# A recurrent cell in four PSUM tiles instead of one, with its seeds copied by halves of the batch

## The chip, the cores and the metric

The kernel runs on one core of a Trainium2 chip. The metric is the time of one execution on the device, in microseconds (us); the median of three runs is quoted. The core has five engines with their own instruction streams, which wait for one another by semaphores: TensorE (PE; its weight loads are listed as PEld), VectorE (DVE), ScalarE (ACT), GpSimd (POOL) and SyncE (SP, which here only issues DMAs). Matmuls write to PSUM, a memory of eight banks of 512 float32 a partition; ACT and DVE read and write it too.

## The reference

A GRU over 128 time steps with a batch of 64 and 512 features, everything in float32; every fourth step (but not the last) the state is passed through a projection before it goes into the next step. The result is added to the input.

```python
def step(h, inp):
    x_t, prop = inp
    comb = concatenate([x_t, h])
    z = sigmoid(comb @ Wz + bz)
    r = sigmoid(comb @ Wr + br)
    h_cand = tanh(concatenate([x_t, r * h]) @ Wh + bh)
    h_new = (1.0 - z) * h + z * h_cand
    h_next = where(prop, tanh(h_new @ Wp + bp), h_new)   # prop: (t + 1) % 4 == 0 and t < 127
    return h_next, h_new
out = x + transpose(ys)                                  # ys: the h_new of all steps
```

## The kernel before

Each weight matrix of 1024 rows is split: the upper 512 rows (`wx`) meet the input x, the lower 512 (`wh`) meet the state. The x part does not depend on the recurrence. It is computed ahead, for groups of four steps and three gates at once, by two nested levels of a fast matrix product with seven multiplications in place of eight: GpSimd forms the sums of inputs (`sum_raw12`, `sum_s12`, `sum_s34` and so on) and recombines the products (`outer_...`) into `cp`, with bias; PE multiplies into four PSUM banks `scratch_q`, `scratch_r`, `scratch_a`, `scratch_x`; ACT (line 466) and DVE (lines 475 to 482) read those out. `G[t]` is the part of `cp` that belongs to step t.

The recurrent part of a step goes into PSUM. The batch of 64 is cut into two halves of 32 (`S = 2`), and the 512 features into four column groups of 128 (`NQ = 4`) which lie on the four quarters of the 128 partitions: one half of one gate is a block of 128 partitions x 128 columns. `gate(i, lT, w)` runs one gate: for each half, four slices of the contraction and four column groups, so 16 matmuls a half. In the profile each of these float32 matmuls counts as two, so a gate is 64 matmuls and 64 weight loads.

Before PE runs a gate, ACT has copied the x part of that step into the place in PSUM on which the matmuls accumulate: `seed(i, t)` (line 364). For the projection the bias takes that part (line 680). Where a gate lies within `rec`, one tile over four banks, is said by `pair(i)`: r in banks 0 and 2 (one bank a half), first 128 columns; the projection in the same two banks, next 128 columns; the candidate in banks 1 and 2, third 128 columns; z with both halves in bank 3.

The order of all engines' work is written out by hand (`manual_schedule`); each engine runs its instructions in the order of the program, and the framework adds the waits, from what each instruction reads and writes of each tile. A step of the loop over t does, in this order:

1. r: `gate(R, ...)`, then `read_out()` of scratch banks that are complete; for each half a sigmoid in place (line 658), r times h on DVE (659), a transpose to `rhT` on DVE (227); then `seed(R, t + 1)` for the next step.
2. z: `gate(Z, ...)`, sigmoid to SBUF (670) and 1 - z in place (671), `keep` = (1 - z) h on DVE (672), `seed(Z, t + 1)`, and before a projection the bias into its place (680).
3. `fill(places[0])`: so many units of the x part from `queue`, each 16 matmuls and 16 weight loads in the profile's count.
4. candidate: `gate(H_, rhT, ...)`, `read_out()`; for each half tanh in place (703), times z (704), plus keep to `h_new` (713), transpose to `hT` (227); then `seed(H_, t + 1)`, and `fill(places[1])`.
5. in projection steps: `gate(P_, ...)`, tanh (729) and transpose for each half.
6. GpSimd's sums for the x part, and the addition of h_new to the input (780), from where SP stores it.

How many units go into the two fills repeats every eight steps (98 units in all), with exceptions at the head and tail:

```python
PLACES = (
    (8, 3, 0), (3, 8, 0), (6, 8, 0), (6, 8, 0), (6, 4, 0), (4, 6, 0), (8, 6, 0), (8, 6, 0),
)
```

In the last six steps the first fill is empty and the second has five units at most; there the x part of the last two steps is computed plainly, from weights that are loaded again (`reload`).

Of the kernel before, what the change touches and what calls it, by code (L numbers as in the profile page):

```python
# [9 lines left out]
F32 = mybir.dt.float32  # L10
BF16 = mybir.dt.bfloat16
U16 = mybir.dt.uint16
AF = mybir.ActivationFunctionType
# [4 lines left out]
def kernel(  # L18
# [14 lines left out]
    nc = tc.nc  # L33
    B, T, D = x.shape
    H = h0.shape[1]
    P = 128
    S = 2
    V = B // S
    NQ = P // V
    J = H // NQ  # L40
    C = 2
# [5 lines left out]
    R, Z, H_ = range(3)  # L47
# [11 lines left out]
    two = ctx.enter_context(tc.tile_pool(name="two", bufs=2))  # L59
    ps_c = ctx.enter_context(tc.tile_pool(name="ps_c", bufs=1, space=PSUM))  # L60
# [19 lines left out]
    def part(q):  # L80
        return slice(q * V, (q + 1) * V)
# [16 lines left out]
    xr = {}  # L98
# [5 lines left out]
    bias_in = const.tile([P, 4, J], F32, name="bias")  # L104
# [11 lines left out]
    for h in range(S):  # L116
        nc.gpsimd.dma_start(
            out=h_init[:, h, :],
            in_=h0[ts(h, V), :].rearrange("b (q j) -> q b j", q=NQ),
# [22 lines left out]
    for q in range(NQ):  # L142
        nc.sync.dma_start(
            out=bias_in[part(q), 3, :],
            in_=bp[ts(q, J)].rearrange("(o n) -> o n", o=1).broadcast_to([V, J]),
# [1 line left out]

    rec = ps_c.tile([P, 4, 4 * J], F32, name="rec")  # L150

    def pair(i):
        if i == Z:
            return rec[:, 3, : S * J].rearrange("p (h n) -> p h n", h=S)
        if i == H_:
            return rec[:, 1:3, 2 * J : 3 * J]
        first = 0 if i == R else J
        return rec.rearrange("p (h two) n -> p h two n", two=2)[:, :, 0, first : first + J]

    P_ = 3  # L160
    scratch = [ps_c.tile([P, 4 * J], F32, name=f"scratch_{n}") for n in "qrax"]
    q_ps, r_ps, a_ps, x_ps = (
        s[:, : 3 * J].rearrange("p (m h v) -> p m h v", m=2, h=S) for s in scratch
    )

    bias = bias_in.rearrange("p i (c n) -> p c i n", c=C)

    def halves(ps):
        return ps.rearrange("p h (c n) -> p h c n", c=C)

    def spread(bank, rows, which):
        bank = bank.rearrange("p (i n) -> p i n", i=4)
        n = len(which)
        for q in range(NQ):
            nc.tensor.matmul(
                bank[part(q), 0:n, :],
                lhsT=ones,
                rhs=bias_row[:, rows, ts(q, J)],
                start=True,
                stop=True,  # L180
            )
        for j, i in enumerate(which):
            nc.scalar.copy(bias_in[:, i, :], bank[:, j, :])
# [4 lines left out]
    def idle(n):  # L188
        for i in range(n):
            nc.tensor.matmul(  # L190
                rec[part(i % NQ), i // NQ % 4, :],
                lhsT=zeros[:, :V],
                rhs=zeros,
                start=True,
                stop=True,
            )

    def products(ps, lhs, rhs, start=False):
        for q in range(NQ):
            nc.tensor.matmul(  # L200
                ps[part(q)],
                lhsT=lhs,
                rhs=rhs(q),
                start=start,
                stop=True,
                skip_group_check=True,
            )

    def gate(i, lT, w):
        for h in range(S):  # L210
            for k in range(K):
                products(
                    pair(i)[:, h, :], lT[:, h, ts(k, V)], lambda q: w[:, k, ts(q, J)]
                )

    def product(ps, lT, w, k, start=False):
# [9 lines left out]
    def turn(dst, src):  # L226
        nc.vector.transpose(out=dst, in_=src)  # L227

    def new_T(tag, name):
        return two.tile([P, S, P], F32, tag=tag, name=name)  # L230
# [123 lines left out]
    G = {}  # L354
# [5 lines left out]
                G[2 * q + b] = cp[q][:, :, b]  # L360

    def seed(i, t):
        if t < T:
            nc.scalar.copy(halves(pair(i)), G[t][:, :, :, i, :].rearrange("p c h n -> p h c n"))  # L364

    queue = []
    pending = []
# [1 line left out]
    def fill(n):  # L369
        for _ in range(min(n, len(queue))):  # L370
            unit, end = queue.pop(0)
            unit()
            if end is not None:
                pending.append(end)

    def read_out():
        while pending:
            pending.pop(0)()
# [185 lines left out]
    }  # L564

    idle(64)
    join_x(0, 0)
    idle(16)
    join_x(0, 1)
    idle(32)  # L570
    h = h_init
    hT = new_T("hT", "hT_init")
    both = [plain(0), plain(1)]
    for e in range(3):
        parts = [us[4 * e : 4 * e + 4] for us in both]

        queue.extend(sum(map(list, zip(*parts)), []) if e == R else sum(parts, []))
        fill(4)
        if e == H_:
            read_out()  # L580
            for i in range(3):
                seed(i, 0)
        fill(4)
        if e == R:
            spread(scratch[3], slice(0, 2), (R, H_))
            spread(scratch[1], slice(2, 3), (Z,))
            nc.gpsimd.tensor_sub(bias_d, bias[:, 1, 0:3, :], bias0)
        if e == Z:
            for half in range(S):
                turn(hT[:, half, :], h[:, half, :])  # L590
    read_out()
    for i in (1, 2, 3):
        sum_inner(i, nc.gpsimd)
# [1 line left out]
    for t in range(T):  # L595
        g, j = divmod(t, Q4)
# [23 lines left out]
        def join(n):  # L620
            if t == 0:
                join_x(0, 2 + n)
            elif t == 1:
                join_x(1, 2 + n)
            elif t == 2:
                join_x(2, n)
            elif t == 4:
                join_x(3, 2 * n)
                join_x(3, 2 * n + 1)
            elif duo >= 0 and u in (5, 6):  # L630
                join_x(even + 2, 2 * (u - 5) + n)
            elif duo >= 1 and u in (1, 3):
                join_x(odd, u - 1 + n)

        gate(R, hT, wh[R])
        if t == 1:
            for i in (5, 7):
# [15 lines left out]
            outer_u2(odd - 2)  # L653
        rh = two.tile([P, S, J], F32, tag="rh", name=f"rh_{t}")
        rhT = new_T("rhT", f"rhT_{t}")
        for half in range(S):
            r = pair(R)[:, half, :]
            nc.scalar.activation(r, r, AF.Sigmoid)  # L658
            nc.vector.tensor_mul(rh[:, half, :], r, h[:, half, :])  # L659
            turn(rhT[:, half, :], rh[:, half, :])  # L660
        if t != 3:
            seed(R, t + 1)
        if last:
            seed(H_, t)
        join(0)

        gate(Z, hT, wh[Z])
        z = two.tile([P, S, J], F32, tag="z", name=f"z_{t}")
        keep = two.tile([P, S, J], F32, tag="keep", name=f"keep_{t}")
        nc.scalar.activation(z, pair(Z), AF.Sigmoid)  # L670
        nc.scalar.activation(pair(Z), pair(Z), AF.Sigmoid, scale=-1.0)  # L671
        nc.vector.tensor_mul(keep, pair(Z), h)  # L672
        join(1)
        if t == 1:
            sum_raw34(1)
# [1 line left out]
            seed(R, t + 1)  # L677
        seed(Z, t + 1)
        if prop:
            nc.scalar.copy(  # L680
                pair(P_), bias_in[:, 3, :].unsqueeze(1).to_broadcast([P, S, J])
            )
        if last:
            nc.gpsimd.tensor_add(xr[g][:, j], xr[g][:, j], keep)
        if t == 0:
# [8 lines left out]
        if t == T - 7:  # L694
            reload()

        gate(H_, rhT, wh[H_])
        read_out()
        h_new = two.tile([P, S, J], F32, tag="h", name=f"h_{t}")
        hT = None if last else new_T("hT", f"hT_{t}")  # L700
        for half in range(S):
            c = pair(H_)[:, half, :]
            nc.scalar.activation(c, c, AF.Tanh)  # L703
            nc.vector.tensor_mul(c, c, z[:, half, :])  # L704
            if last:
                o = xr[g][:, j, half, :]
                nc.vector.tensor_add(o, c, o)
                (nc.sync, nc.scalar)[half].dma_start(
                    out=out[ts(half, V), t, :].rearrange("b (q n) -> q b n", q=NQ),
                    in_=o,  # L710
                )
                continue
            nc.vector.tensor_add(h_new[:, half, :], c, keep[:, half, :])  # L713
            turn(hT[:, half, :], h_new[:, half, :])
        if t < T - 2:
            seed(H_, t + 1)
        h = h_new
# [5 lines left out]
        if prop:  # L723
            gate(P_, hT, wp)
            read_out()
            h = two.tile([P, S, J], F32, tag="hprop", name=f"hprop_{t}")
            hT = new_T("hT", f"hpT_{t}")
            for half in range(S):
                nc.scalar.activation(h[:, half, :], pair(P_)[:, half, :], AF.Tanh)
                turn(hT[:, half, :], h[:, half, :])  # L730
            fill(places[2])
        if t == 0:
            join_x(1, 0)
# [48 lines left out]
        n = 0  # L782
        if t >= T - CHUNK:
            n = 3 if t == T - 2 else 0
        elif j == Q4 - 1:
            n = 4
        if n:
            for half in range(S):
                for q in range(NQ):
                    nc.sync.dma_start(  # L790
                        out=out[ts(half, V), t - n + 1 : t + 1, ts(q, J)],
                        in_=xr[g][part(q), j - n + 1 : j + 1, half, :],
                    )
        if j == 1 and g >= 1 and (g + 1) * Q4 < T:
            new_xr(g + 1)
# [47 lines left out]
```

## Time and profile before

| What | Value |
|---|---|
| Median of three runs | 1789.92 us (1787.52 to 1790.38) |
| Profiled execution: its time, its span | 1789.36 us, 1787.6 us |
| PE busy; its weight loads | 1378.8 us (77%), 51,920 matmuls; 1273.5 us (71%), 51,920 |
| DVE, ACT, POOL busy | 786.7 us (44%), 529.6 us (30%), 884.0 us (49%) |
| Mean granted clock of PE | 0.980 |
| Chain that ended last | PE 64%, DVE 14%, ACT 11%, issue 5%, rest 6% |
| Program of PE, fetched by DMA queue 8 | 406 packets, 6.65 MB |
| z activation (line 670) of steps 0, 8 and 120 | starts at 63.48, 189.82 and 1689.48 us |

The span is the time from the first to the last instruction of the profiled execution. A busy share is that of the whole span, and engines work side by side; a line like "L364" is a line of the kernel. "Idle before" is the time that an engine stood still ahead of an instruction, with the engine and line that ended the wait; "issue" means that the profile shows nothing that the engine waited for. Up to step 0's z the weights are still being loaded; from step 8 to step 120 the pattern of eight steps repeats fourteen times.

### The profile page before, as it was taken

Reading aid. Unit: us, or ns where it says so; the run is one execution under the profiler, and the core shown is the slowest. Engines: PE = TensorE matmul, PEld = TensorE weight load, DVE = VectorE, ACT = ScalarE, POOL = GpSimd, SP = SyncE. Lnnn points to the kernel's source line nnn. Section 1 sums busy time; section 2 is a strip of 40 time slices with the busy share of each in tenths; the row PEclk is TensorE's granted clock in tenths of the full one; section 3 lists DMA queues with packets and bytes.
Section 4 is the critical chain, followed back from the end, with each engine's and each line's share of the span. In section 5 each row is a group of like instructions: output and inputs, shape, how many; then the busy total and the mean of one; then the engine's idle time right before and its main releaser. Section 6 shows DMA issues by size and latency. Waiting matters only on the chain.

```text
span 1787.6 us, 111363 instructions
## 1 busy us (share of the span) xinstructions
PE 1378.8 (77%) x51920; PEld 1273.5 (71%) x51920; DVE 786.7 (44%) x2163; ACT 529.6 (30%) x1571; POOL 884.0 (49%) x1030
## 2 busy tenths in 40 slices
PE   6678777778777778777777777778787788777765
PEld 4577767777777777777777777777777777777755
DVE  0444444444444445444444444444444444444423
ACT  0123333233333333333333233333333323333221
POOL 2366555465454555545555554545545555454310
PEclk7799999999999999999999999999999999999999
DMA  2301111101111110111111111110111101111020
GB/s 103 110 24 39 39 28 40 38 17 38 39 39 28 38 31 26 39 29 50 28 29 34 32 39 28 39 39 16 40 28 50 28 24 32 40 27 28 16 79 14
DMA packets 114219, 66.36 MB, mean 37 GB/s; under 512 B 12604, under 2 KB 108988, under 8 KB 113756
## 3 DMA queue, kind: packets, MB, share of 16 engines
q1 hardware_dynamic: 113048, 58.90, 11.9%
q8 instruction: 406, 6.65, 1.5%
q14 instruction: 57, 0.47, 0.1%
q10 hardware_dynamic: 452, 0.20, 0.0%
q0 software_dynamic: 256, 0.14, 0.0%
HBM read 42.41 MB, written 16.78 MB: 33 GB/s over the span
## 4 chain that ended last, share of the span: by engine, by line
PE 64%; DVE 14%; ACT 11%; issue 5%; SPq 3%; DMA 2%; POOL 1%; ACTq 0%; DVEq 0%; POOLq 0%
PE rec L200 44%; PE scratch_x L200 5%; PE scratch_r L200 5%; PE scratch_q L200 5%; ACT rec L364 5%; DVE rh L659 4%; PE scratch_a L200 4%; SPq L93 2%; DVE rec L704 2%; DVE h L713 2%; DVE rhT L227 2%; ACT rec L658 2%; DVE keep L672 1%; DVE hT L227 1%; ACT rec L703 1%
## 5 line engine op out<-in xcount | busy, mean ns | idle before, releaser
L200 PE MATMUL rec<-wh,hT 128*32 128x128 f32 x12288 | 393.1, 278 | 200.3 <-ACT rec L364 187.9
L200 PEld LDWEIGHTS rec<-wh,hT 128*32 128x32 f32 x12288 | 337.3, 111 | 241.4 <-ACT rec L364 221.5
L200 PE MATMUL rec<-wh,rhT 128*32 128x128 f32 x8192 | 255.7, 274 | 33.0 <-ACT rec L364 22.6
L200 PEld LDWEIGHTS rec<-wh,rhT 128*32 128x32 f32 x8192 | 224.4, 110 | 46.7 <-ACT rec L364 29.7
L780 POOL TENSOR_TENSOR xr<-xr,h 128x256 f32<-128x256 f32 x127 | 92.4, 727 | 311.2 <-DVE h L713 286.9
L364 ACT COPY rec<-cp 128x256 f32<-128x256 f32 x384 | 144.6, 377 | 218.4 <-DVE h L713 87.1
L200 PE MATMUL rec<-wh,hpT 128*32 128x128 f32 x3968 | 121.5, 274 | 82.3 <-ACT rec L364 55.3
L200 PEld LDWEIGHTS rec<-wh,hpT 128*32 128x32 f32 x3968 | 105.4, 110 | 98.2 <-ACT rec L364 63.7
L510 POOL TENSOR_TENSOR cp<-mb,mb 128x768 f32<-128x768 f32 x75 | 136.6, 1821 | 65.4 <-DVE mb L482 61.8
L510 POOL TENSOR_TENSOR mb<-mb,mb 128x768 f32<-128x768 f32 x58 | 105.3, 1816 | 128.2 <-DVE mb L482 128.2
L672 DVE TENSOR_TENSOR keep<-rec,h 128x256 f32<-128x256 f32 x96 | 40.8, 425 | 278.7 <-ACT rec L671 278.7
L703 ACT ACTIVATE rec<-rec 128x128 f32<-128x128 f32 x256 | 67.1, 262 | 311.7 <-PE rec L200 217.3
L658 ACT ACTIVATE rec<-rec 128x128 f32<-128x128 f32 x256 | 67.1, 262 | 302.1 <-PE rec L200 256.4
L514 POOL TENSOR_TENSOR mb<-mb,bias 128x768 f32<-128x768 f32 x35 | 63.8, 1822 | 175.2 <-DVE mb L482 175.2
L670 ACT ACTIVATE z<-rec 128x256 f32<-128x256 f32 x128 | 49.1, 384 | 291.5 <-PE rec L200 291.5
L704 DVE TENSOR_TENSOR rec<-rec,z 128x128 f32<-128x128 f32 x256 | 76.7, 300 | 114.8 <-ACT rec L703 114.8
L466 ACT COPY cq<-scratch_q 128x384 f32<-128x384 f32 (+1 forms) x214 | 101.4, 474 | 22.5 <-PE scratch_q L200 22.1
L475 DVE TENSOR_TENSOR cx<-scratch_r,cx 128x384 f32<-128x384 f32 (+1 forms) x107 | 59.3, 554 | 98.1 <-ACT cx L466 98.1
L659 DVE TENSOR_TENSOR rh<-rec,h 128x128 f32<-128x128 f32 x192 | 56.0, 292 | 94.1 <-ACT rec L658 94.1
L510 POOL TENSOR_TENSOR cp<-cp,mb 128x768 f32<-128x768 f32 x29 | 53.0, 1829 | 87.7 <-DVE mb L482 86.6
L480 DVE TENSOR_TENSOR mb<-scratch_r,cq 128x384 f32<-128x384 f32 (+1 forms) x107 | 59.3, 554 | 79.9 <-ACT cq L466 62.0
L510 POOL TENSOR_TENSOR cp<-mb 128x768 f32<-128x768 f32 x47 | 85.9, 1827 | 12.3 <-ACT rec L364 10.9
(134 smaller groups left out, 2606.5 us busy)
## 6 DMA issues: line engine op xcount, KB each, us to landing
out_dram<-xr SPq DMA_DIRECT2D x249, 64.0 KB
xr<-in_x_dram SPq DMA_DIRECT2D x248, 64.0 KB
xs<-in_x_dram SPq DMA_DIRECT2D x240, 64.0 KB
wx<-in_L_cond_Wr_dram SPq DMA_DIRECT2D x7, 256.0 KB
wx<-in_L_cond_Wz_dram SPq DMA_DIRECT2D x7, 256.0 KB
wx<-in_L_cond_Wh_dram SPq DMA_DIRECT2D x7, 256.0 KB
wh<-in_L_cond_Wr_dram SPq DMA_DIRECT2D x4, 256.0 KB
wh<-in_L_cond_Wz_dram SPq DMA_DIRECT2D x4, 256.0 KB
```

The costliest lines, as they stand in the source:

```text
L200: nc.tensor.matmul(ps[part(q)], lhsT=lhs, rhs=rhs(q), start=start, stop=True, skip_group_check=True,)
L364: nc.scalar.copy(halves(pair(i)), G[t][:, :, :, i, :].rearrange("p c h n -> p h c n"))
L466: nc.scalar.copy(c[:, :nm], ps[:, :nm])
L475: nc.vector.tensor_add(T2[n][:, :nm], r_ps[:, :nm], T2[n][:, :nm])
L480: nc.vector.tensor_add(blocks(0, 1), runs(r_ps[:, :nm]), runs(q2[:, :nm]))
L510: nc.gpsimd.tensor_add(dst, a, b)
L514: nc.gpsimd.tensor_add(m, m, v.unsqueeze(1).to_broadcast([P, 4, 3, J // 2]))
L658: nc.scalar.activation(r, r, AF.Sigmoid)
L659: nc.vector.tensor_mul(rh[:, half, :], r, h[:, half, :])
L703: nc.scalar.activation(c, c, AF.Tanh)
L704: nc.vector.tensor_mul(c, c, z[:, half, :])
L780: nc.gpsimd.tensor_add(xr[g][:, j], xr[g][:, j], h_new)
```

## The change

The four banks of `rec` become four tiles, one bank each: `rec_r0` and `rec_r1` hold r (first columns) and the projection (next columns) of halves 0 and 1, `rec_h` the candidate of half 0, `rec_z` both halves of z. The candidate of half 1 lies in the third columns of `rec_r1`. So the layout in the banks is what it was. An instruction can now name one tile only, so the seeds of r, candidate and projection, which wrote both halves in one copy of 128x256, become two copies of 128x128, one a half; z's seed stays one copy. The order of the work is otherwise the same; the loop variable `half` is renamed `s_` in many places, which is left out here.

```diff
-    rec = ps_c.tile([P, 4, 4 * J], F32, name="rec")
-
-    def pair(i):
+    rec = [ps_c.tile([P, 4, J], F32, name=f"rec_{n}") for n in ("r0", "r1", "h", "z")]
+    zz = rec[3][:, :S]
+    P_ = 3
+
+    def half(i, h):
         if i == Z:
-            return rec[:, 3, : S * J].rearrange("p (h n) -> p h n", h=S)
+            return zz[:, h]
         if i == H_:
-            return rec[:, 1:3, 2 * J : 3 * J]
-        first = 0 if i == R else J
-        return rec.rearrange("p (h two) n -> p h two n", two=2)[:, :, 0, first : first + J]
-
-    P_ = 3
+            return (rec[2][:, 0], rec[1][:, 2])[h]
+        return rec[h][:, 0 if i == R else 1]
...
                 products(
-                    pair(i)[:, h, :], lT[:, h, ts(k, V)], lambda q: w[:, k, ts(q, J)]
+                    half(i, h), lT[:, h, ts(k, V)], lambda q: w[:, k, ts(q, J)]
                 )
...
     def seed(i, t):
-        if t < T:
-            nc.scalar.copy(halves(pair(i)), G[t][:, :, :, i, :].rearrange("p c h n -> p h c n"))
+        if t >= T:
+            return
+        src = G[t][:, :, :, i, :].rearrange("p c h n -> p h c n")
+        if i == Z:
+            nc.scalar.copy(zz.rearrange("p h (c n) -> p h c n", c=C), src)
+            return
+        for h in range(S):
+            nc.scalar.copy(half(i, h).rearrange("p (c n) -> p c n", c=C), src[:, h])
...
-        nc.scalar.activation(z, pair(Z), AF.Sigmoid)
-        nc.scalar.activation(pair(Z), pair(Z), AF.Sigmoid, scale=-1.0)
-        nc.vector.tensor_mul(keep, pair(Z), h)
+        nc.scalar.activation(z, zz, AF.Sigmoid)
+        nc.scalar.activation(zz, zz, AF.Sigmoid, scale=-1.0)
+        nc.vector.tensor_mul(keep, zz, h)
...
         if prop:
-            nc.scalar.copy(
-                pair(P_), bias_in[:, 3, :].unsqueeze(1).to_broadcast([P, S, J])
-            )
+            for s_ in range(S):
+                nc.scalar.copy(half(P_, s_), bias_in[:, 3, :])
```

More of the change, by code (lines that the diff above doesn't have):

```diff
@@ L166 @@
     bias = bias_in.rearrange("p i (c n) -> p c i n", c=C)
-    def halves(ps):
-        return ps.rearrange("p h (c n) -> p h c n", c=C)
     def spread(bank, rows, which):
@@ L190, in idle @@
             nc.tensor.matmul(
-                rec[part(i % NQ), i // NQ % 4, :],
+                rec[i // NQ % 4].rearrange("p c n -> p (c n)")[part(i % NQ)],
                 lhsT=zeros[:, :V],
@@ L588 @@
         if e == Z:
-            for half in range(S):
-                turn(hT[:, half, :], h[:, half, :])
+            for s_ in range(S):
+                turn(hT[:, s_, :], h[:, s_, :])
     read_out()
@@ L655 @@
         rhT = new_T("rhT", f"rhT_{t}")
-        for half in range(S):
-            r = pair(R)[:, half, :]
+        for s_ in range(S):
+            r = half(R, s_)
             nc.scalar.activation(r, r, AF.Sigmoid)
-            nc.vector.tensor_mul(rh[:, half, :], r, h[:, half, :])
-            turn(rhT[:, half, :], rh[:, half, :])
+            nc.vector.tensor_mul(rh[:, s_, :], r, h[:, s_, :])
+            turn(rhT[:, s_, :], rh[:, s_, :])
         if t != 3:
@@ L679 @@
         if prop:
-            nc.scalar.copy(
-                pair(P_), bias_in[:, 3, :].unsqueeze(1).to_broadcast([P, S, J])
-            )
+            for s_ in range(S):
+                nc.scalar.copy(half(P_, s_), bias_in[:, 3, :])
         if last:
@@ L700 @@
         hT = None if last else new_T("hT", f"hT_{t}")
-        for half in range(S):
-            c = pair(H_)[:, half, :]
+        for s_ in range(S):
+            c = half(H_, s_)
             nc.scalar.activation(c, c, AF.Tanh)
-            nc.vector.tensor_mul(c, c, z[:, half, :])
+            nc.vector.tensor_mul(c, c, z[:, s_, :])
             if last:
-                o = xr[g][:, j, half, :]
+                o = xr[g][:, j, s_, :]
                 nc.vector.tensor_add(o, c, o)
-                (nc.sync, nc.scalar)[half].dma_start(
-                    out=out[ts(half, V), t, :].rearrange("b (q n) -> q b n", q=NQ),
+                (nc.sync, nc.scalar)[s_].dma_start(
+                    out=out[ts(s_, V), t, :].rearrange("b (q n) -> q b n", q=NQ),
                     in_=o,
@@ L712 @@
                 continue
-            nc.vector.tensor_add(h_new[:, half, :], c, keep[:, half, :])
-            turn(hT[:, half, :], h_new[:, half, :])
+            nc.vector.tensor_add(h_new[:, s_, :], c, keep[:, s_, :])
+            turn(hT[:, s_, :], h_new[:, s_, :])
         if t < T - 2:
@@ L727 @@
             hT = new_T("hT", f"hpT_{t}")
-            for half in range(S):
-                nc.scalar.activation(h[:, half, :], pair(P_)[:, half, :], AF.Tanh)
-                turn(hT[:, half, :], h[:, half, :])
+            for s_ in range(S):
+                nc.scalar.activation(h[:, s_, :], half(P_, s_), AF.Tanh)
+                turn(hT[:, s_, :], h[:, s_, :])
             fill(places[2])
@@ L787 @@
         if n:
-            for half in range(S):
+            for s_ in range(S):
                 for q in range(NQ):
                     nc.sync.dma_start(
-                        out=out[ts(half, V), t - n + 1 : t + 1, ts(q, J)],
-                        in_=xr[g][part(q), j - n + 1 : j + 1, half, :],
+                        out=out[ts(s_, V), t - n + 1 : t + 1, ts(q, J)],
+                        in_=xr[g][part(q), j - n + 1 : j + 1, s_, :],
                     )
```

## The prediction

> **What bounds the kernel now.** I read the waits first, then one step in the timeline, then the instruction traffic. On PE the longest wait by far is for the copies that seed the recurrent banks (line, who is waited for, us in total, times, longest):
>
> ```profile
> PE rec L200 <- ACT rec L364: 302.2, 215, 2.1
> ACT rec L703 <- DVE h L713: 93.5, 127, 0.8
> ACT rec L658 <- DVE rh L659: 45.7, 128, 0.4
> ```
>
> The second and third lines say that the sigmoid or tanh of half 1 waits until VectorE is done with half 0, though the halves lie in different columns. One step in order of time (start, duration, engine, line, what, idle time before it):
>
> ```profile
> 900.20 1.96 PE L200 MATMUL rec<-wh,hT 128*32 128x128 f32 x64
> 902.28 0.26 ACT L658 ACTIVATE rec<-rec 128x128 f32<-128x128 f32 x1 [1.28 <-PE rec L200]
> 902.57 0.29 DVE L659 TENSOR_TENSOR rh<-rec,h 128x128 f32<-128x128 f32 x1 [0.97 <-ACT rec L658]
> 902.90 0.26 ACT L658 ACTIVATE rec<-rec 128x128 f32<-128x128 f32 x1 [0.36 <-DVE rh L659]
> 903.19 0.29 DVE L659 TENSOR_TENSOR rh<-rec,h 128x128 f32<-128x128 f32 x1
> 903.52 0.38 ACT L364 COPY rec<-cp 128x256 f32<-128x256 f32 x1 [0.36 <-DVE rh L659]
> 903.95 1.95 PE L200 MATMUL rec<-wh,hT 128*32 128x128 f32 x64 [1.79 <-ACT rec L364]
> ```
>
> The first sigmoid starts only after all 64 matmuls of r, although half 0 had ended after 32 of them. Then everything that touches `rec` runs in single file, and the z matmuls at 903.95, whose columns are in another bank and whose input hT was ready before r, wait for the seed of the next step's r. So `rec` is waited for as one thing. Tiles allocated apart are not: ACT copies out of scratch_q while PE writes scratch_r:
>
> ```profile
> 907.37 0.51 PE L200 MATMUL scratch_r<-wx,s 128*32 128x96 f32 x16
> 907.49 0.47 ACT L466 COPY cq<-scratch_q 128x384 f32<-128x384 f32 x1
> ```
>
> Next, eight steps (one period of `PLACES`), between two first sigmoids (us, then busy time and count of each engine):
>
> ```profile
> 878.44:984.48 106.04, 83.14 (x3232) 77.60 (x3232) 49.14 (x135) 33.45 (x99) 56.50 (x66) 1.00 0.14 36
> ```
>
> PE works 83 of 106 us; nobody else is above 57. What then stops PE from closing up is in the page's part 3 (packets, MB, share of 16 DMA engines):
>
> ```profile
> q8 instruction: 406, 6.65, 1.5%
> ```
>
> That is PE's program: 51,920 matmuls and as many weight loads in 406 packets, so 256 instructions a packet. The trace already shows PE halting ("issue") where it has run densely for a few us, and the halts are 128 matmuls (one packet) apart. Looking for a gap over 0.2 us exactly at a packet's first instruction I find about 90, and 24 times two in succession: the packet between took 3.41 to 4.02 us, 3.65 on average. These are some (stretch, length, PE busy and count):
>
> ```profile
> 962.36:965.83 3.47, 3.27 (x129) 1.00 0.02 5
> 1057.61:1061.35 3.74, 3.27 (x128) 1.00 0.34 93
> 1286.17:1289.64 3.47, 3.22 (x129) 1.00 0.02 5
> 1652.19:1655.96 3.77, 3.16 (x127) 1.00 0.02 4
> ```
>
> **The change, part by part.** *Waits.* With four tiles, z's bank no longer waits for the seed of r, and half 0 no longer for half 1. I lay a step out by the rows above, with W the first matmul of r, a gate 2.0 us (half 1.0), 0.08 from PE to ACT, 0.04 between other engines, ACT 0.26, DVE 0.30, transpose 0.31. r of half 0 ends W+1.0, its transpose is done at W+2.05; half 1 W+2.0 and W+3.05; the seeds of r follow rh, the last done at W+3.0. z runs W+2.0 to 4.0 with no wait (its seed is a step old). Then come the `places[0]` fill units (32 instructions, 0.33 us each: 0.66 for 64), so h half 0 starts at W+4.0 at the earliest, with its input 1.9 us old. The candidate's half 0 ends at Y-1.0 (Y the end of that gate), its tanh at -0.66, product, sum and transpose at Y+0.35; half 1 at Y+1.4. `places[1]` covers that: three units already give Y+1.0 for r's half 0 and Y+2.0 for half 1. Where three VectorE adds of a batch stand ahead (0.55 each) the chain ends up to 1.5 us later, at Y+2.9 at worst after a step with `places[0]` of 3, and there `places[1]` is 8 (2.6 us) and half 1 is wanted at Y+3.6. In a projection step P's half 0 activation and transpose (0.7 us) lie beside its half 1. So PE loses no wait in a full step.
>
> *The shared bank.* r1 holds r, P and the candidate of half 1, so the candidate's half 1 waits for the seeds there: of r W+3.0; of P, after z's two activations, keep and seed (X+1.75, X the end of z), X+2.3. It is wanted at X+1.0 plus the fill: in full steps with P the fill is 8 or 6 units, 2.0 us or more. Cost nothing; without that fill (one P step of the tail) 1.3.
>
> The Trainium skill, PSUM — Partial Sum Buffer ("PSUM bank collisions raise a hardware error"), says to guard by bank and not by address, which speaks against three gates in one bank; by it the price is the 1.3 us just named, and no run here shows a gate in a bank of its own.
>
> *Copies.* A seed of 128x256 takes 377 ns; two of 128x128 by the row of the same size (262) take 524, so 147 more, for r and candidate each step and P each fourth: 18 in eight steps, 2.6 us on ACT, which is then busy 36 of 93. ACT works ahead of PE by over 1 us where these stand; uncovered, they would cost their 0.15 each. No DMA, no POOL instruction and no matmul is added or moved. POOL's tightest delivery I find is s (done 918.47, read by PE at 923.88): 5.4 us, of which PE's gaps between (0.72, 1.85 and 0.42) go, so 2.4 stay.
>
> *What is late next.* Gates 26 x 2.0 and 98 units x 0.33 are 84.4 us for eight steps. The program of these steps is 6464 instructions, 25.3 packets; at 3.65 us that is 92.2. I expect PE to be paced by its instruction packets. A packet of fill runs 2.6 us and would wait, one of gates runs 4.0 and would not; most hold both, so I take the average (kept wholly apart, 13 x 4.0 + 12.3 x 3.65 would be 97). Some 4 more PE wait instructions a step add 0.13 packet, 0.5 us: 93 us per eight steps. Between the ends 3.41 (87 us) and 4.02 (102) I take the mean of the 24, since the regime is the same one made permanent.
>
> The Trainium skill, Runtime: NRT & Kernel Launch ("Instruction fetch mechanics"), calls the cost of crossing from one block of instructions to the next "mostly hidden". By it the eight steps would take 84.4 and the whole some 1440; the halts above differ, and I go by them.
>
> *Sum.* The profiled run took 1789.36 us, with a span of 1787.6 (the median of the three runs is 1789.92, 0.03% more). Between the z activations of step 8 (189.82) and step 120 (1689.48) lie 14 periods, 107.1 us each: 14 x (107.1 - 93) = 198 saved. Head (63.5 to 189.8): 30.6 packets at 3.65 are 112 of its 126, but loads hold it until 72 and POOL is on its chain from 110 to 136; between 0 and 14, I take 8. Tail (98.1 us): the last six steps have no first fill and up to five units; by the layout above a step takes 7.1 to 7.7 (10.4 with P) for 11.4 to 15.4 now, and ends when the chain of half 1 does. Step 120 and 121 at 11.5 and 10.7, then 7.4, 10.4, 7.1, 7.7, 7.1, 7.3: 69, plus an allowance of 2 for the reloaded weights: 27 saved. Together 233: 1556 us.
>
> **The rivals.** (A) The forecast: PE is paced by packets at 3.5 to 3.85 us: 89 to 98 per period, 1500 to 1630. (B) The packets come ahead after all; for it: three quarters of the boundaries show no gap; against: the gaps come just where PE has run densely, and elsewhere a wait for a seed gave the fetch its time. 85 us per period, 14 x 22.1 and 39 in head and tail, 349 saved: 1440. (C) Fetching slows as other transfers are squeezed into less time (of the rows shown, the one beside 93 GB/s took 3.74 and those at 5 GB/s 3.47, though one at 4 took 3.77): 3.95, near the longest pair, gives 100.3 per period, 14 x 6.8 and 35, 130 saved: 1659. (D) The other side, and the change not doing what it says: the four tiles are waited for as one. Then nothing is saved and each seed on the path is two copies, 0.15 us longer: before z 128 times, before r or P some 100 times: 34 us, 1823. Against it stands the scratch row above. It decides if z's matmuls still follow the seed of r; and A itself turns over at 4.2 us per packet, where 25.3 packets fill today's 106.
>
> **How the numbers follow.** A 0.77, B 0.07, C 0.11, D 0.05. The time is A's, 1556; A's ends hold most of its 0.77, and reaching half way to B and to C's 1659 brings the range to 1470 to 1660. About 0.2% (4 us) can be told from no change: faster 0.94, same 0.01 (C at its worst), slower 0.05.
>
> **What would show it.** Right: the line "PE rec <- ACT rec L364" falls from 302 us to under 20; z's matmuls follow r's directly; the first sigmoid starts about 1.1 us after r's first matmul; eight steps take 89 to 98 us with PE busy near 83; "issue" becomes PE's largest wait, at every packet; q8 still near 406 packets. Wrong: PE waiting for ACT or DVE once a step (D, or a wait on r1), POOL's sums arriving after PE asks, or eight steps under 87 (B).

## The result and the profile after

The changed kernel takes 1574.98 us (median of four runs, 1573.8 to 1575.51); the kernel before, beside it, 1788.77 (1787.52 to 1790.38). The ratio is 0.880, 95% interval 0.879 to 0.882: 12% faster. The profiled execution took 1573.8 us. In two later comparisons, on other chips, the same changed kernel took 0.892 and 0.900 of before; the first experiment shows where that time goes. Every ratio below is to runs of before in the same comparison.

From the page of the changed kernel: the span; busy time of each engine; PE's program (packets, MB, share of 16 DMA engines); the chain that ended last, by engine.

```profile
span 1572.0 us, 111797 instructions
...
PE 1369.3 (87%) x51920; PEld 1261.9 (80%) x51920; DVE 776.7 (49%) x2163; ACT 561.7 (36%) x1858; POOL 885.4 (56%) x1030
...
q8 instruction: 407, 6.67, 1.8%
...
PE 83%; issue 11%; SPq 3%; DMA 2%; POOL 1%; ACT 0%; DVE 0%; POOLq 0%; DVEq 0%; ACTq 0%
```

PE does the same work in nearly the same busy time as before (1378.8 us there); ACT and DVE, together 25% of the chain before, are gone from it, and "issue" has risen from 5% to 11%. PE's waits (us in total, times, longest):

```profile
PE rec_r L197 <- issue: 51.1, 92, 1.4
PE scratch_q L197 <- issue: 26.4, 42, 1.2
PE scratch_x L197 <- issue: 23.4, 42, 1.1
PE scratch_r L197 <- issue: 22.5, 47, 1.0
PE rec_h L197 <- issue: 18.5, 28, 1.5
PE rec_z L197 <- issue: 9.9, 24, 0.8
...
PE scratch_a L197 <- issue: 8.1, 20, 0.8
...
PE rec_r L197 <- ACT rec_r L684: 2.3, 2, 1.2
```

The 302 us of waiting for a seed of a gate are down to nothing. What is left are 160 us of "issue", in which PE is not seen to wait for any engine, spread over whatever PE happens to run. The last line is the one wait on a seed that remains: the candidate's half 1 waits twice (at 119 and at 1536 us) for the projection's seed, in the bank that r, projection and candidate share. Places in one step (start, duration, what, idle before):

```profile
844.81 1.96 PE L197 MATMUL rec_r<-wh,hT 128*32 128x128 f32 x64
...
845.93 0.26 ACT L661 ACTIVATE rec_r<-rec_r 128x128 f32<-128x128 f32 x1 [1.00 <-PE rec_r L197]
...
846.56 0.61 PE L197 MATMUL rec_z<-wh,hT 128*32 128x128 f32 x14
...
847.32 1.58 PE L197 MATMUL rec_z<-wh,hT 128*32 128x128 f32 x49
...
851.34 0.57 PE L197 MATMUL scratch_x<-tt,s 128*32 128x96 f32 x17 [0.84 <-issue]
855.13 0.60 PE L197 MATMUL scratch_x<-tt,o 128*32 128x96 f32 x18 [0.52 <-issue]
859.34 0.74 PE L197 MATMUL rec_r<-wh,hT 128*32 128x128 f32 x18 [1.04 <-issue]
```

The sigmoid of r's first half starts 1.12 us after r does, while PE is at the second half; z's matmuls begin at 846.56, as r ends, and not after a seed. The breaks at 847.32, 851.34, 855.13 and 859.34 are some 4 us apart, in a gate, in input products and in r: they follow the count of instructions, not the kind of work. Take every 256th instruction of PE (matmuls, weight loads and semaphore instructions in order of time), the first of each packet: at 360 of some 407 such boundaries it starts over 0.2 us after the instruction before it, 260 us in sum; before there were 94, with 63 us. Call a packet limited if it has such a gap at both ends. There are 327, and they take 3.74 us on average, from 3.3 to 4.35.

The transfers of queue 8 show what PE waits for. In a limited packet the transfer of the next one starts 1.25 us after the packet's first instruction and takes 1.10 us, and PE goes on 1.39 us after the transfer's end (means; the last lies between 1.23 and 1.56 in nine of ten). At the 310 boundaries of the kernel before that have no gap, the packet had been there longer: its transfer had ended 2.8 us ahead (median). So a limited packet lasts until its successor has come: 1.25 us until the successor's transfer starts, and 2.5 us from there.

Stretches from z of step 0 to z of step 8, from there to z of step 120, and to the end (us; busy time and count of PE, PEld, DVE, ACT, POOL; granted clock; DMA share; GB/s):

```profile
63.48:179.92 116.44, 101.23 (x3918) 94.98 (x3914) 61.01 (x158) 35.34 (x118) 75.53 (x87) 0.99 0.18 52
179.92:1501.99 1322.07, 1171.30 (x45201) 1086.61 (x45195) 679.37 (x1891) 498.20 (x1641) 783.87 (x910) 1.00 0.14 38
1501.99:1572.00 70.01, 60.05 (x2171) 56.56 (x2170) 30.69 (x98) 23.74 (x87) 13.05 (x12) 0.99 0.20 61
```

1322.07 / 14 = 94.43 us per eight steps, of which PE is busy 83.7 (1171.30 / 14).

### The profile page after: what moved, and what is told of

It reads as the page before. It is cut to its first block, busy times and chain, and to the rows that moved or that the text cites. A ratio compares the mean times of both kernels' runs of the same rounds, so it can differ in the third digit from the quotient of the medians.

```text
span 1572.0 us, 111797 instructions
## 1 busy us (share of the span) xinstructions
PE 1369.3 (87%) x51920; PEld 1261.9 (80%) x51920; DVE 776.7 (49%) x2163; ACT 561.7 (36%) x1858; POOL 885.4 (56%) x1030
## 3 DMA queue, kind: packets, MB, share of 16 engines
q1 hardware_dynamic: 113048, 58.90, 13.5%
## 4 chain that ended last, share of the span: by engine, by line
PE 83%; issue 11%; SPq 3%; DMA 2%; POOL 1%; ACT 0%; DVE 0%; POOLq 0%; DVEq 0%; ACTq 0%
PE rec_r L197 27%; PE rec_z L197 15%; PE scratch_x L197 10%; PE scratch_q L197 10%; PE scratch_r L197 10%; PE rec_h L197 7%; PE scratch_a L197 5%; SPq L93 3%; DMA wh<-in_L_cond_Wh_dram 1%; DMA wh<-in_L_cond_Wr_dram 1%; DMA xr<-in_x_dram 0%; POOL cp L513 0%; POOL mb L517 0%; DVE keep L675 0%; ACT z L673 0%
## 5 line engine op out<-in xcount | busy, mean ns | idle before, releaser
L197 PE MATMUL rec_r<-wh,hT 128*32 128x128 f32 x6144 | 206.7, 273 | 32.4 <-issue 31.8
L197 PE MATMUL rec_z<-wh,hT 128*32 128x128 f32 x6144 | 207.7, 273 | 11.5 <-issue 9.9
L197 PEld LDWEIGHTS rec_r<-wh,hT 128*32 128x32 f32 x6144 | 176.7, 110 | 44.3 <-issue 43.2
L197 PEld LDWEIGHTS rec_z<-wh,hT 128*32 128x32 f32 x6144 | 180.3, 110 | 22.7 <-issue 22.1
L197 PE MATMUL rec_h<-wh,rhT 128*32 128x128 f32 x4096 | 156.0, 273 | 21.8 <-issue 18.5
L197 PE MATMUL rec_r<-wh,rhT 128*32 128x128 f32 x4096 | 157.4, 273 | 15.7 <-issue 12.7
L661 ACT ACTIVATE rec_r<-rec_r 128x128 f32<-128x128 f32 x256 | 67.1, 262 | 248.9 <-PE rec_r L197 248.9
L197 PEld LDWEIGHTS rec_h<-wh,rhT 128*32 128x32 f32 x4096 | 123.5, 110 | 31.5 <-issue 26.3
L197 PEld LDWEIGHTS rec_r<-wh,rhT 128*32 128x32 f32 x4096 | 127.0, 110 | 24.0 <-issue 20.1
L367 ACT COPY rec_r<-cp 128x128 f32<-128x128 f32 x384 | 102.7, 268 | 103.7 <-DVE h L715 68.9
```

Of the source, the lines that this page charges most:

```text
L197: nc.tensor.matmul(ps[part(q)], lhsT=lhs, rhs=rhs(q), start=start, stop=True, skip_group_check=True,)
L367: nc.scalar.copy(half(i, h).rearrange("p (c n) -> p c n", c=C), src[:, h])
```

## The experiments

Theory: the four tiles took the waits for seeds away, and PE is now paced by its instruction packets; its own matmuls have time to spare. Rivals: PE's work itself is the bound; a chain of waits between gates still is; the gain is not from the tiles but could be had by order alone.

**The changed kernel again, on two other chips** (after_again, after_beside; no edit).

> The changed kernel as it is, on the chip of the experiments that follow. From the ratio 0.880 of its first comparison: 0.878 to 0.883 of before, some 1580 us where before takes 1794. Its use is the step: 14 periods of eight steps of 94.4 us each, about 360 of some 407 packet boundaries with a gap of over 0.2 us on TensorE.

> The changed kernel beside the next three runs. It took 0.880 of before where it was first compared and 0.900 in the comparison with rz_merged, where a limited packet took 3.83 us in place of 3.72; so 0.875 to 0.905 here, 1570 to 1625 us, and lower the shorter the packet is: 1 us of time per eight steps for each 0.04 us (25.3 packets).

Measured: 1614.01 us, ratio 0.900 (0.896 to 0.903); and 1605.47, ratio 0.892 (0.889 to 0.895). The first lies above what was expected of it (1580). The kernel before hardly differs between the comparisons (1789 to 1801). The table sets the mean time of a limited packet beside the time of eight steps; its parts are the start of the next packet's transfer, the transfer, and the time from its end to PE's next instruction.

| Comparison | Gaps at boundaries | Limited packets | us each | of these: start, transfer, to PE | x 25.3 | eight steps |
|---|---|---|---|---|---|---|
| first | 360 | 327 | 3.74 | 1.25, 1.10, 1.39 | 94.7 | 94.4 |
| after_beside | 372 | 346 | 3.82 | 1.31, 1.12, 1.39 | 96.7 | 96.2 |
| after_again | 376 | 357 | 3.87 | 1.33, 1.15, 1.39 | 98.0 | 97.5 |

The fourteen periods of after_again:

```profile
183.75:1549.14 1365.39, 1172.52 (x45201) 1086.13 (x45195) 679.92 (x1891) 498.34 (x1641) 785.36 (x912) 1.00 0.14 36
```

PE's work is the same (83.8 us for 83.7); what grew is the packet's time, in the start and the length of the transfer. The last two columns agree in good part because they must: most packets are limited. That the fetch sets the pace, and is not merely as long, is for the next two experiments to show. Why it is slower in one comparison than in another stays open. The expectations speak of packets of 3.72 and 3.83 us: the fourteen periods give 3.72 and 3.84 if gaps of over 1.2 us are left out. There is no ground for that, since at 23 of the first comparison's 24 such gaps PE is not seen to wait for any engine either.

The kernel before has a gap at a quarter of its boundaries only, and so hardly feels it.

**Thinner matmuls, same instructions** (thin_gates, repeated beside the changed kernel as thin_beside).

```diff
-                    half(i, h), lT[:, h, ts(k, V)], lambda q: w[:, k, ts(q, J)]
+                    half(i, h)[:, : J // 2], lT[:, h, ts(k, V)],
+                    lambda q: w[:, k, q * J : q * J + J // 2],
```

> The changed kernel with every recurrent gate and projection computed over 64 of its 128 columns a block (the other half of those products is left out). The number of PE instructions and all waits stay. Theory 1 (packets of instructions pace PE): the same time as the changed kernel, 1560 to 1580 us. Rival (PE is paced by the running of its matmuls): a gate of 2.0 us falls to 1.2 or less, 26 gates in eight steps, so some 20 us per eight steps and about 1290 us in all.

> As thin_gates (gates and projection over 64 of their 128 columns, the other half of these products left out; the same instructions), now beside the changed kernel on one chip. Packets pace TensorE: within 2% of the changed kernel, though TensorE's busy time is 340 us shorter. If the matmuls' own time counted, 150 us or more below it.

Measured: 1598.91 us, ratio 0.891 (0.888 to 0.894); and 1602.71, ratio 0.890 (0.886 to 0.894), against 0.892 (0.889 to 0.895) for the changed kernel beside it: no difference. (The first lies above its 1560 to 1580, which came from the first comparison's 1575.) From the page of the second run:

```profile
PE 1037.7 (65%) x51920; PEld 947.1 (59%) x51920; DVE 761.1 (47%) x2163; ACT 561.3 (35%) x1858; POOL 883.1 (55%) x1030
...
PE 59%; issue 32%; SPq 3%; DMA 2%; POOL 1%; DVE 1%; ACT 1%; ACTq 0%; POOLq 0%; DVEq 0%
```

A quarter of PE's busy time is gone, over 330 us, and "issue" has taken nearly all of it. A limited packet takes 3.81 us here and 3.82 in the changed kernel beside it, and eight steps 96.8 and 96.2, though PE is busy in only 62.7 of the 96.8. What a matmul does is not what paces PE; that it is an instruction is.

**More instructions, next to no work** (more_instr). The tile of zeros, whose buffer was used again, also gets one that stays.

```diff
+        for i in range(64):
+            nc.tensor.matmul(
+                rec[3][part(i % NQ), 3, 0:8], lhsT=zeros[:, :V], rhs=zeros[:, :8],
+                start=False, stop=True, skip_group_check=True,
+            )
         gate(Z, hT, wh[Z])
```

> The changed kernel with 64 tiny matmuls of zeros (8 columns) more a step, ahead of z, into columns that nothing reads: 128 instructions, half a packet, with hardly any data. Theory 1: half of 3.7 us a step in 128 steps, 225 to 240 us more, about 1810 us. Rival (the running of matmuls paces): 64 pairs at no more than the 20 ns that a pair of fill takes, so at most 165 us more and by their width far less, 1590 to 1740.

Measured: 1847.42 us, ratio 1.030 (1.027 to 1.033): the whole gain of the change is lost, more than the 1810 us expected. The program of PE, and the fourteen periods:

```profile
q8 instruction: 471, 7.72, 1.8%
```

```profile
198.79:1769.47 1570.68, 1252.75 (x52382) 1158.85 (x52376) 681.06 (x1891) 499.54 (x1640) 781.62 (x907) 1.00 0.12 32
```

Eight steps took 112.2 us, and PE was busy in 89.5 of them. 457 of some 471 boundaries show a gap, and a limited packet took 3.83 us. In thin_gates, on the same chip, it took 3.79 and eight steps 96.0: 25.3 + 4 packets of 3.79 us are 111.1 of the 112.2. So a packet costs about the same whether it holds the kernel's matmuls or, in part, these. The 1810 went by 3.7 us a packet and by the time of the first comparison.

**Fewer instructions, the same columns** (rz_merged). r and z multiply the same h, so their weights go into one tile and a matmul takes 128 columns of each.

```diff
-    wh = [const.tile([P, K, H], F32, name=f"wh_{i}") for i in range(3)]
+    whrz = const.tile([P, K, 2, H], F32, name="wh_rz")
+    wh = [whrz[:, :, 0], whrz[:, :, 1], const.tile([P, K, H], F32, name="wh_2")]
...
+    def gate_rz(lT):
+        for h in range(S):
+            for k in range(K):
+                products(
+                    rec[h][:, 0:2, :], lT[:, h, ts(k, V)], lambda q: whrz[:, k, :, ts(q, J)]
+                )
...
-        if i == Z:
-            return zz[:, h]
         if i == H_:
-            return (rec[2][:, 0], rec[1][:, 2])[h]
-        return rec[h][:, 0 if i == R else 1]
+            return rec[2 + h][:, 0]
+        return rec[h][:, {R: 0, Z: 1, P_: 2}[i]]
```

From step 1 on `gate_rz` stands in place of the two gates; z, 1 - z and `keep` are made by halves, and one copy of 128x256 seeds r and z of a half.

> r and z read the same h, so their weights go into one tile and one matmul computes 128 columns of each (256 columns, the same number of columns in all): 128 instructions a step fewer, four packets fewer in eight steps. The four PSUM tiles become two with r, z and projection of one half of the batch each, and two with a half of the candidate each; keep and the seeds are made by halves. Theory (packets pace TensorE): 25.3 - 4 = 21.3 packets of 3.72 us are 79 us per eight steps, less than the 84 us that the matmuls take now; TensorE's own work becomes the bound and a period takes 85 to 91 us in place of 94.4. 14 periods save 50 to 130 us; the tail, which has no other work to put behind r, loses up to 10. Together 1450 to 1535, most likely 1480. Rival 1 (the gaps are not the instructions' but the chain's from gate to gate): the period stays at 94 or grows, since r of the second half now ends 2 us later in a step: 1575 to 1620. Rival 2 (a matmul of 256 columns runs at a lower rate than two of 128): TensorE's busy time rises above 1400 us and the time stays above 1560.

Measured: 1396.11 us (1394.04 to 1398.72), ratio 0.778 (0.775 to 0.780), against 0.900 for the changed kernel beside it: a further 13.5%, and below all that was expected. Busy times and the program of PE; PE's longest waits; and the fourteen periods:

```profile
PE 1314.7 (94%) x43792; PEld 1159.4 (83%) x43792; DVE 794.3 (57%) x2291; ACT 568.0 (41%) x1988; POOL 887.8 (64%) x1030
...
q8 instruction: 343, 5.62, 1.7%
```

```profile
PE rec_rz L195 <- issue: 11.5, 24, 0.9
PE scratch_q L195 <- issue: 10.8, 20, 1.0
```

```profile
168.93:1327.35 1158.42, 1119.82 (x38040) 995.31 (x38036) 695.12 (x2004) 503.05 (x1752) 787.93 (x915) 1.00 0.16 42
```

64 packets fewer, 82.7 us per eight steps, and PE is busy in 80.0 of them (97%). Gaps at packets fell from 376 (311 us) in the changed kernel beside it to 122 (73 us), and at the other boundaries the packet's transfer had ended 1.9 us ahead (median). The theory said that PE's own work would be the bound, with 21.3 packets at 79 us well below it. But at this comparison's 3.87 us they are 82.4, as long as what was measured: PE's work and its packets are now so close that this run does not tell which of them bounds it. Where the expectation of 1480 was too high: eight steps took 82.7 for the 85 to 91 expected, 32 to 116 us in fourteen; the tail saved 3 us (69 for 72 beside it) where a loss of up to 10 was expected, and the head, of which nothing was said, 14 (106 for 120). PE's work was taken as unchanged, 84 us; it is 80.0. One part is seen in the rows, 62 wide matmuls in 3.62 us, 58 ns each, for two of 30.6 ns (64 in 1.96), about 1.4 us in eight steps; the rest was not told apart.

**z alone in a tile of its own** (z_own, repeated beside the changed kernel as z_own_beside): r, projection and candidate stay in one tile of three banks, seeded whole.

```diff
-    rec = ps_c.tile([P, 4, 4 * J], F32, name="rec")
+    rec = ps_c.tile([P, 3, 4 * J], F32, name="rec")
+    rec_z = ps_c.tile([P, 4 * J], F32, name="rec_z")
```

> One part alone: z in a tile of its own, r, projection and candidate in one tile of three banks, seeds in whole copies. Theory 1 (PE is then paced by its instruction packets, 25.4 per eight steps at 3.7 us): the gap before z goes (2.1 us a step), those left, before r, P and after P, are some 6 us per eight steps and lie mostly beside the fetching: 95 to 98 us per eight steps, about 1617 us in all, so three quarters of the gain. Rival (each wait removed pays for itself, the halves as much as z): half of the gain, about 1680 us.

> As z_own (z in a tile of its own, one three-bank tile for the rest, whole seeds), now beside the changed kernel on one chip: 1615 to 1645 us. What is asked is its share of the change's gain: 75% if the changed kernel takes 1575 here, 90% if it takes 1615. Theory (the packets pace both): the share is 80 to 95%, since what z_own keeps of waits lies under the packets for the most part. Rival (the other waits add to it in full): 70 to 78%.

Measured: 1633.83 us, ratio 0.911 (0.907 to 0.914), nearer to the theory's 1617 than to the rival's 1680; and 1630.93, ratio 0.905 (0.901 to 0.909), beside the changed kernel's 0.892 (0.889 to 0.895). So 0.095 of 0.108: this one separation brings 88% of the gain (82 to 95% from the ends of the intervals), inside the theory's 80 to 95 and outside the rival's 70 to 78. Its waits show why the rest brings little:

```profile
PE rec L201 <- issue: 50.0, 76, 1.4
PE rec L201 <- ACT rec L365: 36.4, 45, 1.5
PE scratch_q L201 <- issue: 28.1, 43, 1.4
PE scratch_r L201 <- issue: 27.2, 51, 1.1
PE rec L201 <- DVE hpT L228: 27.1, 30, 1.1
```

Some 64 us of waits for ACT and DVE remain, but the whole is only 25 us longer: gaps at packets are 222 us in sum, for 291 in the changed kernel beside it. A packet can arrive while PE waits.

**The same cover by order alone** (fill_first): the kernel before, with three units of input products moved ahead of z.

```diff
+        early = 3 if duo >= 0 and t < T - 10 else 0
+        fill(early)
         gate(Z, hT, wh[Z])
...
-        fill(places[0])
+        fill(places[0] - early)
```

> The kernel before, with its one PSUM tile and whole seeds, but in steps 3 to 117 three units of the input products (0.6 us each) are issued ahead of the z gate and three fewer behind it. If the wait that the change removed was only z waiting for the sigmoid of r, its reads and its seed (1.8 us a step), then 1.8 us of work put into it does the same without new tiles: a period falls from 107.1 us towards the packets' pace of 94 and the time to 1600 to 1660 (other waits of the one tile, as r's on the candidate's seed, stay). Rival: the products behind z covered the chain from r to the candidate, so the wait comes back there: the time stays within 2% of before (1760 to 1830).

Measured: 1731.11 us, ratio 0.964 (0.960 to 0.967). Both expectations missed it. The first line is PE's wait for the seeds, 302 us before; the others are one step:

```profile
PE rec L200 <- ACT rec L364: 233.0, 251, 2.0
```

```profile
1021.13 0.84 PE L200 MATMUL scratch_a<-wx,o 128*32 128x96 f32 x32
...
1021.44 0.26 ACT L658 ACTIVATE rec<-rec 128x128 f32<-128x128 f32 x1 [1.73 <-PE rec L200]
...
1021.79 0.51 PE L200 MATMUL scratch_r<-wx,s 128*32 128x96 f32 x16
...
1022.06 0.26 ACT L658 ACTIVATE rec<-rec 128x128 f32<-128x128 f32 x1 [0.36 <-DVE rh L659]
...
1022.74 0.38 ACT L364 COPY rec<-cp 128x256 f32<-128x256 f32 x1 [0.41 <-DVE rh L659]
...
1023.17 1.95 PE L200 MATMUL rec<-wh,hT 128*32 128x128 f32 x64 [0.86 <-ACT rec L364]
...
1026.83 1.69 PEld L200 LDWEIGHTS rec<-wh,rhT 128*32 128x32 f32 x64 [0.27 <-ACT rec L364]
```

Three units are 1.0 us, not 1.8 as the expectation took (0.6 for a unit, which takes 0.33), and halve the wait at z, from 1.8 to 0.86. The units are then missing behind z, where the candidate waits for z's seed in the same tile: more waits, 251 for 215. Work moved between two waits covers one or the other; separate tiles remove both. This is one order of many: that no order alone could do it is not shown.

**The split seeds alone** (copies_only), and the same with work in the wait ahead of z (copies_fill, which adds the edit of fill_first).

```diff
-            nc.scalar.copy(halves(pair(i)), G[t][:, :, :, i, :].rearrange("p c h n -> p h c n"))
+            src = G[t][:, :, :, i, :].rearrange("p c h n -> p h c n")
+            if i == Z:
+                nc.scalar.copy(halves(pair(i)), src)
+                return
+            for h in range(S):
+                nc.scalar.copy(pair(i)[:, h].rearrange("p (c n) -> p c n", c=C), src[:, h])
```

> One part alone: the seeds by halves, all four banks still one tile. If the tile decides, no wait goes and each seed on the path is 0.15 us longer, before z 128 times and before r or P some 100 times: about 1823 us. If the split of the copies were what helps, it would come down towards 1575; if seeds were off the path, 1789.

> copies_only (one PSUM tile, seeds by halves) with three units of the input products moved ahead of z, as in fill_first. copies_only lost 130 us against before where the copies' length gives 34, and its granted clock fell from 0.98 to 0.93. Theory (the clock is halved for want of work on TensorE in the wait ahead of z, and work in that wait keeps it): the clock is 0.975 or more and the time is that of fill_first plus the copies, 0.964 x 1793 + 34 = 1763 (1745 to 1790). Rival (the split copies cost 130 us in whatever order): about 1860, clock near 0.93.

Measured: copies_only 1924.77 us, ratio 1.072 (1.070 to 1.074), four times the loss that the copies' length gives; copies_fill 1791.61, ratio 0.995 (0.992 to 0.997). The mean granted clock (the share of TensorE's full clock) of copies_only was 0.930, with 66 stretches of mostly 3.4 us at half clock after the loading, 231 us together (before: 9, 31 us; the changed kernel: one, at its end). Two gates of it, in the second of which the clock has just fallen:

```profile
895.94 1.96 PE L200 MATMUL rec<-wh,hT 128*32 128x128 f32 x64 [0.74 <-ACT rec L369]
899.94 2.74 PE L200 MATMUL rec<-wh,hT 128*32 128x128 f32 x64 [2.04 <-DVE xT L240]
```

PE's busy time rose from 1378.8 to 1476.3 us, 97 more for the same matmuls, and the span by 131.0. PE's waits together (gaps over 0.15 us) rose by 34 us, 399 to 433, which is what the copies were priced at. The 97 fit the clock: 200 us more at half speed can lengthen PE's work by 100 at most. In copies_fill the clock is back at 0.978; against fill_first (run on another chip) PE is busy 20 us longer (1399.4 for 1379.5) and the span is 60 longer (1789.0 for 1728.5), so 40 are left for the copies and their order. The theory had the clock right and the time (1763) 29 us too low; the rival's 1860 is out. The Trainium skill, TensorE: Matmul & The Clock Gate ("HAM oscillation — how this bites in real kernels"), puts the rule at idle gaps of over some 3.4 us. Here PE's waits for seeds were 2.3 us at the longest, those ahead of z 2.0 on average and those ahead of r 0.46, and the clock still fell time and again; with 1.8 and 0.34 (before) it did 9 times. Which of these waits decides is not shown.

**Without the stores of step 7 to 123** (no_stores): the condition of the stores, `elif j == Q4 - 1:`, gets `and t == CHUNK - 1`. This takes the traffic of the fourteen periods from 36 to 26 GB/s, not to half as the expectation has it.

> The changed kernel without the stores of the output from step 7 to step 123 (those outputs are left out). If a packet of instructions takes longer where data are moved beside it (3.67 us in quiet stretches, 3.74 to 3.81 where over 30 GB/s were moved), half of the traffic gone brings the mean of a limited packet from 3.72 to about 3.69 and the time down by 5 to 15 us (0.3 to 1%). Rival (the traffic and the longer packets only fall together): the packets stay at 3.72 and the time within 3 us of the changed kernel.

Measured: 1605.64 us, ratio 0.895 (0.891 to 0.898), beside the changed kernel's 0.900 (0.896 to 0.903); a limited packet 3.84 us for 3.87. The size is the one expected, but the intervals overlap: not settled. Traffic does not explain the difference between the comparisons, since limited packets beside less than 5 GB/s took 3.68 us in the first and 3.81 in after_again.

## Why the prediction was right

1556 us was predicted, 1470 to 1660; 1575 came, and 1605 and 1614 on the other chips.

- *The waits.* All held: the line of 302 us is gone, z follows r, the first sigmoid is 1.12 us after r's start (1.1 was said). That no wait returns in a full step held as well: all waits of PE for ACT and DVE together are some 6 us.
- *What is late next.* Packets, as forecast: "issue" is PE's largest wait, 360 of some 407 boundaries show it, and and there the packet's transfer had ended only 1.4 us before. The Trainium skill, Runtime: NRT & Kernel Launch ("Instruction fetch mechanics"), calls the cost of such crossings mostly hidden; the estimate by that was 1440. The trace decides against it, and thin_beside shows it without PE's work in the way.
- *The step that was mis-sized: the packet's time.* 3.65 us was the mean of 24 packets in the trace of before. It was 3.74, and with it 25.3 packets take 94.7, for 92.2. The period was 94.43 instead of 93: 14 x 1.43 = 20 us, which less the 3 us gained more in head and tail is the miss of 17.8 to within 1 us. A mean of 24 with a scatter of 0.2 us is uncertain by 0.04 (an estimate), and the count used here finds one more in the trace of before, of 4.22 us, which makes the mean 3.68; what makes up the rest is not shown. Of the ways a packet could be slower, (C)'s traffic is weak here: 3.68 us below 5 GB/s and 3.82 above 30, where (C) needs 3.95 on average. That the price differs from one comparison to the next, by 0.13 us, was not thought of: the 1605 and 1614 us lie inside the range, but 49 and 58 above the forecast.
- *Instructions.* 4 more waits a step were allowed for, 0.5 us; the trace has 2.4 more semaphore instructions a step on PE (310 in all), and the program grew by one packet. This hid a part of the error above.
- *Head and tail.* 126.3 to 116.4, 9.9 saved for the 8 taken; 98.1 to 70.0, 28.1 for 27. The layout of the tail's steps, drawn from durations of before, was good to 1 us.
- *Copies and the shared bank.* A half seed takes 268 ns (262 was used), and ACT is busy 36 of 94 us. The shared bank's 1.3 us, forecast for one step of the tail, came twice, in head and tail: 2.3 us together, the wait on L684. The Trainium skill, PSUM — Partial Sum Buffer ("PSUM bank collisions raise a hardware error"), says to guard by bank; here that cost these 2.3 us. z does have a bank of its own, before and after; what is not measured is one each for r, projection and candidate.
- *Rivals.* (B) is out by the waits at packets and by the period (94.4 us for 85), (D) by the seeds' waits that are gone. (D)'s price was wrong: split copies into tiles waited for as one are what copies_only runs, 1925 us and not 1823. The 34 us of copies are in it; the clock was left out of the sum, though the profile of before, at 0.980 and with nine half-speed stretches, stood close to it.

## What to carry to other kernels

When a wait is taken off a dense stream of small matmuls, look for the next bound in the count of instructions: here 256 instructions came every 3.7 to 3.9 us on average where PE waited for them, and the count of packets, at a price read from a few places in the trace of before, gave the time of eight steps to 2% in the first comparison and to 5% in the slowest. Then the lever is fewer, wider instructions (r and z as one matmul: a further 13.5%), not less arithmetic (a quarter less PE time: nothing). And of several separations of a tile try first the one whose wait recurs in every step: z's alone brought 88%.

## What the runs showed of the hardware that was not expected

- A packet of PE's program that PE had to wait for took 3.74 us: 1.25 until the next one's transfer began, 1.10 for its 16 KB, 1.39 from its end to PE's next instruction. The last was 1.39 in all three comparisons.
- The same program's limited packets took 3.74, 3.82 and 3.87 us on average in three comparisons, and the changed kernel 1575, 1605 and 1614 us, while the kernel before stayed within 1789 to 1801.
- Waits of 2.0 us ahead of z and 0.46 ahead of r, in place of 1.8 and 0.34, went with a granted clock of 0.930 for 0.980 and 97 us more of PE's busy time, nearly three times what the copies themselves cost.
- Matmuls of 256 columns took 58 ns each in a run of 62, those of 128 columns 30.6 ns in a run of 64, each with its own weight load: for the same columns the wider ones take no longer and are half as many instructions.
